# An attention kernel's filler scheduler: a work budget per step replaced by even rates for two engines

## The chip, the cores and the metric

One core of a Trainium2 chip. The metric is the device time of one launch of the whole program in microseconds, as the median of several runs. The engines are TensorE (PE in the profile; PEld is its weight load), VectorE (DVE), ScalarE (ACT), GpSimd (POOL) and SyncE (SP, whose queue SPq issues nearly all DMAs). Each engine runs its instructions in the order in which the program gives them.

## The reference

Two decoder layers over x of 4 batches, 512 tokens and 256 channels, each block added to x, with a second input ctx of 1024 tokens and 128 channels:

```python
x = x + L0_attn(ln(x))            # q, k softmaxed, 64 landmarks
x = x + L0_xattn(ln(x), ctx)      # (softmax(causal qk) v + softmax(cross qk) v) @ Wp
x = x + L0_ffn(ln(x))             # linear, x and W rounded to 6-bit floats in blocks of 32
x = x + L1_attn(ln(x))            # hyperbolic: -arccosh(..)^2 scores, causal, spike mask
x = x + L1_xattn(ln(x), ctx)      # y = ln(x); y += mha(y, y, causal); y = ln(y); y + mha(y, ctx)
x = x + L1_ffn(ln(x))             # 8 experts, top 2 of a softmax gate
# mha: 16 heads of 32; x + o @ li1, then + gelu(ln(.) @ li2) @ li3
```

In L0_xattn the heads are 16 wide. In L1_xattn the causal mask is laid on after the softmax, so its row sums run over all keys. The gate takes the two largest of 8 experts per token, and normalises their two scores.

## The kernel before, in words

Tokens lie on the 128 partitions, in 16 tiles for all batches; NT = 4 tiles per batch. The stages follow one another: L0_attn and the preparation of ctx (to about 200 us), **stream 0** (l0_xattn, L565), the hyperbolic attention (l1_attn, L985), **stream 1** (l1_xattn, L1210), the expert slots (Slots, L1656), and a last gather and sum.

Both streams are run by class Stream (L305). It has a list of units: one unit is four heads of one batch and one kind of attention, 32 units in each stream. A unit has two passes, both made of tiles of 128 by 512 scores in PSUM. In the first, the d tiles (d_tile, L355), TensorE computes scores with queries on the partitions (L363) and VectorE takes their row maxima (L367, L371, L375); for units marked norm ScalarE also sums exponentials (L379). In the second, the a tiles (a_tile, L394), TensorE computes the scores again, transposed and with the maxima taken in (a bias matmul, L391, or a changed query), and ScalarE writes the exponentials (L399). One step later the outputs multiply them by the values (L491 to L501). A step t is four heads of one d tile of one unit and one a tile of an earlier unit. Stream 0's units are cross attention (full) and causal; stream 1's are causal ones of the first block (marked norm; their mask is laid by GpSimd on the exponentials, L413) and full ones of the second. PSUM is a ring of seven score tiles and one output tile.

**Other work** is laid between the steps: everything that prepares a unit (layer norms ln_pieces, transposes flip, projections feats and values) or follows from one. In stream 0 that is also L0_ffn and the front of the hyperbolic attention (class Front, L737: scaled, binade, nearest and ties round to 6 bits; tokens L867 are the q, k, v projections; squares L888 to series L937 are cosh and sinh by exponentials and a power series on VectorE; lift L951 and turn L955 transpose them, and SP stores them for the next stage). In stream 1 it is li1, mid, flip, li2 (eight pieces), gelu and li3 (four pieces) of each batch and block, then leave, and from leave a gate chain per batch (gate, L1531: scores, choose, choose2, choose3, rank, four scatters of two indirect DMAs each on GpSimd (L1624), biases). After the last unit it is the first expert slots.

A piece is a tuple (earliest step, due step, least number of steps after the one before it, cost, function), and pieces stand in chains, which keep their order. In a step, `run` (L503) does in this order: force (L346) lays all pieces that are due, then come the step's tiles and outputs, then the functions put off by `after` (L324), then fill (L339) lays ready pieces, earliest due first, as long as the costs spent in this step are under a budget: 1.8 in stream 0 and 3.0 in stream 1, roughly microseconds of TensorE. What force laid counts; what `after` laid does not. Most of Front's VectorE pieces cost 0.

**Slots.** 39 slots of 128 routed tokens. Slot s needs its weights (2052 KB, fetch_w L1776) and its rows (fetch_z L1770); the rows of slots 0 to 15 (NEARLY) are loaded ahead, those of later slots in fetch. Four weight buffers. round (L1832) gives for each slot s: fetch(s + 3) with cost 0, two halves of hidden(s + 1), turn(s + 2), output(s) with a store on SP. The chain of slots 13 and later, which begins with fetch(16), is added by `rest` (L1404), just behind the scatters of the last gate, due at 10**6:

```python
s.chain([(s.t, 10**6, 0, c, f) for c, f in slots.rest()])          # L1405
if s + 3 < NSLOT:
    work.append((0.0, lambda s=s: self.fetch(s + 3)))
```

## Time and profile before

| | |
|---|---|
| median of 3 runs | 3500.57 us (3499.15 to 3501.44) |
| profiled execution, its own time | 3504.81 us |
| its span, first to last instruction | 3503.1 us |
| mean granted TensorE clock | 0.910 of full |
| VectorE, ScalarE, GpSimd busy | 2115.4, 1902.3, 781.9 us |
| stream 0, 200 to 1143 us: PE, DVE, ACT, POOL busy | 913.9, 664.3, 468.6, 154.6 us |
| stream 1, 1715 to 3133 us: PE, DVE, ACT, POOL busy | 1332.0, 855.6, 867.3, 204.1 us |
| slots, 3133 to 3450 us: PE busy, DMA share | 312.4 us, 0.76 |
| weights of a slot, issue to landing | 7.5 / 9.0 / 16.2 us (least, median, most) |

How to read it. A busy line gives an engine's busy time, its share of the span and its instructions. The rows of slices cut the span in 40 equal parts, one digit each, the busy share in tenths; PEclk is the clock that TensorE was granted, in tenths. The chain that ended last is followed back from the last instruction, and its shares say on which engine the time was spent. A timeline row has start, duration, engine, line, operation, output and inputs, and in brackets the idle time of the engine just before it and what released it. A line "x8" is eight instructions taken together, and matmuls of one row overlap, since their ends are modelled.

### The profile page before, as it was taken

What the parts mean: (1) busy time and instruction counts of PE and PEld (TensorE: products, weight loads), DVE (VectorE), ACT (ScalarE), POOL (GpSimd) and SP (SyncE); (2) the same over time, 40 slices, a digit from 0 to 9 for tenths busy, and PEclk for the clock granted to TensorE, in tenths of its full rate; (3) what the DMA queues carried; (4) which work ended last, traced back from release to release, by engine and by line L of the source; (5) the groups of instructions that cost most, each with busy time, mean ns of one, the idle gap of its engine ahead of it and who ended that gap; (6) DMA issues with size and microseconds to landing.
All of it is one profiled execution on the core that took longest, in us unless ns stands there. A gap on an engine that the chain in (4) does not pass through costs nothing.

```text
span 3503.1 us, 50666 instructions
## 1 busy us (share of the span) xinstructions
PE 3081.6 (88%) x19095; PEld 1514.7 (43%) x19095; DVE 2115.4 (60%) x5076; ACT 1902.3 (54%) x3845; POOL 781.9 (22%) x667
## 2 busy tenths in 40 slices
PE   6789999999999667677899989999999998989994
PEld 3433333333333334344434444433343343448994
DVE  4576676776776687876667564565657656433112
ACT  2225555454454765779587676556555664533331
POOL 1010112112122665668211220110101101021003
PEclk9779999999999667788789999999999999989997
DMA  8100000000000200020000000000000000035885
GB/s 281 57 26 7 1 7 1 14 24 4 28 1 14 71 13 32 25 98 7 25 1 1 1 1 19 7 1 31 1 13 9 11 1 13 7 145 203 317 328 166
DMA packets 81397, 176.08 MB, mean 50 GB/s; under 512 B 6264, under 2 KB 63744, under 8 KB 76032
## 3 DMA queue, kind: packets, MB, share of 16 engines
q1 hardware_dynamic: 76016, 161.16, 13.0%
q0 software_dynamic: 3072, 8.39, 0.8%
q8 instruction: 150, 2.46, 0.3%
q10 hardware_dynamic: 2064, 3.29, 0.3%
q14 instruction: 95, 0.78, 0.1%
HBM read 127.48 MB, written 45.34 MB: 49 GB/s over the span
## 4 chain that ended last, share of the span: by engine, by line
PE 67%; DVE 13%; ACT 10%; issue 5%; POOL 3%; DMA 3%; SPq 0%; POOLq 0%; ACTq 0%; DVEq 0%
PE ps_s L363 16%; PE ps_g L494 7%; PE ps_s L398 5%; PE ps_s L1802 4%; PE ps_s L1809 4%; PE ps_s L1401 3%; PE ps_s L1331 3%; PE ps_s L1385 3%; PE ps_s L636 3%; PE ps_s L391 2%; ACT pt L399 2%; ACT ps_s L379 2%; PE ps_s L1120 2%; PE ps_s L1372 2%; PE ps_g L501 2%
## 5 line engine op out<-in xcount | busy, mean ns | idle before, releaser
L399 ACT ACTIVATE pt<-ps_s 128x512 f32<-128x512 f32 (+2 forms) x1536 | 791.3, 570 | 758.8 <-PE ps_s L398 645.0
L363 PE MATMUL ps_s<-kT,qT 32*128 32x512 f32 (+3 forms) x3072 | 941.0, 633 | 38.1 <-ACT pt L399 12.7
L375 DVE TENSOR_REDUCE mx<-ps_s 128x1 f32<-128x512 f32 x768 | 490.4, 685 | 239.8 <-PE ps_s L363 136.8
L363 PEld LDWEIGHTS ps_s<-kT,qT 32*128 32x128 f32 x3072 | 322.9, 189 | 337.8 <-issue 121.8
L398 PE MATMUL ps_s<-qa,kT 32*128 32x512 f32 (+3 forms) x1536 | 447.9, 604 | 3.1 <-DVE mx L375 1.7
L367 DVE TENSOR_REDUCE mx<-ps_s 128x1 f32<-128x512 f32 x512 | 328.4, 685 | 166.1 <-PE ps_s L363 162.8
L398 PE MATMUL ps_s<-qT,kT 32*128 32x512 f32 x1536 | 421.9, 642 | 0.0
L379 ACT ACTIVATE ps_s<-ps_s,mx 128x512 f32<-128x512 f32 x512 | 341.2, 670 | 33.5 <-DVE mx L367 33.1
L1080 POOL TENSOR_TENSOR s<-s,mh 128x1280 f32<-128x1280 f32 x64 | 187.1, 2948 | 68.3 <-ACT mh L1079 52.4
L1804 ACT ACTIVATE hid<-ps_s,we 128x128 f32<-128x128 f32 x312 | 89.0, 370 | 199.0 <-issue 103.8
L164 POOL TENSOR_TENSOR ln_r<-ln_ve,mhalf 128x4 f32<-128x4 f32 x40 | 41.0, 1024 | 620.1 <-DVE ln_ve L159 556.4
L371 DVE CUSTOM_DVE_ANT_0 junk<-ps_s,dmask 128x512 f32<-128x512 f32 (+3 forms) x256 | 125.7, 491 | 88.2 <-PE ps_s L363 44.9
L391 PE MATMUL ps_s<-qm,all 3*128 3x512 bf16 x768 | 164.3, 391 | 12.6 <-ACT ps_s L379 10.8
L398 PEld LDWEIGHTS ps_s<-qa,kT 32*128 32x128 f32 x1536 | 148.8, 189 | 51.5 <-DVE mx L375 30.9
L1063 PE MATMUL ps_s<-qk 32*128 32x256 f32 (+3 forms) x512 | 102.2, 601 | 64.3 <-DVE mh L1068 57.5
L1802 PE MATMUL ps_s<-zsT,we 128*128 128x128 f32 x1248 | 149.2, 279 | 7.4 <-DVE zsT L1793 6.5
L1802 PEld LDWEIGHTS ps_s<-zsT,we 128*128 128x128 f32 x1248 | 147.9, 195 | 10.9 <-DVE zsT L1793 7.4
L1095 POOL TENSOR_TENSOR s<-s 128x1280 f32<-128x1280 f32 x64 | 147.6, 2339 | 12.3 <-ACT s L1091 12.3
L1120 PE MATMUL ps_s<-ident,s 128*128 128x128 f32 x640 | 129.1, 339 | 19.0 <-ACT s L1114 17.9
L1122 DVE COPY pt<-ps_s 128x512 f32<-128x512 f32 x160 | 108.6, 689 | 56.4 <-PE ps_s L1120 56.2
L1809 PE MATMUL ps_s<-we,hid 128*128 128x256 f32 x624 | 141.0, 379 | 0.0
L494 PE MATMUL ps_g<-pt,v 128*32 128x512 f32 x1024 | 140.4, 619 | 0.0
(439 smaller groups left out, 5096.9 us busy)
## 6 DMA issues: line engine op xcount, KB each, us to landing
we<-in_we SPq DMA_DIRECT2D x39, 2052.0 KB, 9.0
rows<-zero SPq DMA_DIRECT2D x8, 2048.0 KB, 17.0
qk_d<-qkT SPq DMA_DIRECT2D x32, 256.0 KB, 2.5
qk<-qk_d SPq DMA_DIRECT2D x8, 1024.0 KB, 6.6
zs<-rows SPq DMA_DIRECT2D x39, 128.0 KB, 3.7
outs<-ys SPq DMA_DIRECT2D x39, 128.0 KB, 3.7
li<-in_a_li SPq DMA_DIRECT2D x4, 1024.0 KB, 8.2
v_d<-vp SPq DMA_DIRECT2D x16, 143.5 KB, 1.8
```

The costliest lines, as they stand in the source:

```text
L363: PE.matmul(ps[:, 0:n], u.qT[r, ts(qt)], u.kT[r, hf * 512 : hf * 512 + n], start=True, stop=True)
L367: V.tensor_reduce(m, ps[:, 0:n], AX.X, ALU.max, negate=True)
L375: V.tensor_reduce(m, ps[:, 0:n], AX.X, ALU.max)
L379: S.activation(ps, ps, AF.Exp, bias=m, accum_out=sm)
L391: PE.matmul(ps, self.ones[r, :], u.qm[r, :], start=True, stop=False)
L398: PE.matmul(ps[:, c0:], u.kT[r, ts(kt)], (u.qa if u.first_row else u.qT)[r, c0:], start=u.first_row, stop=True)
L399: S.activation(u.pt[:, j, c0:], ps[:, c0:], AF.Exp, scale=u.scale)
L494: PE.matmul(o[r, c0:], u.v(kt, j), pt[:, j, c0:], start=first, stop=last)
L1080: G.tensor_add(s, s, m)
L1120: PE.transpose(ps[:, ts(j)], u.s[h // 2][:, h % 2, c0 : c0 + P], ident)
L1802: PE.matmul(ps[:, ts(f)], u.w[:, k : k + P], u.zT[:, c, :], start=c == 0, stop=c == 1)
L1809: PE.matmul(ps[:, 0:C], u.h[:, f, :], u.w[:, 2048 + f * C : 2048 + f * C + C], start=f == 0, stop=f == 7)
```

## The change

The budget is gone. A cost now has a sign: positive is microseconds of TensorE, negative of VectorE. At each step with score tiles, rates computes for each of the two engines the largest of (work due by d) / (steps to d + 1) over all due steps d; in steps without score tiles both rates are 3.0. fill lays a ready piece if it costs 0, if its engine has spent nothing in this step, or if half of it still fits under its engine's rate. force and `after` count what they lay. chain pulls the due steps of earlier pieces back to those of later ones. The costs are set anew (Front's VectorE pieces get theirs; scores from 2.0 to 3.4; scatter from 0.2 to 0), many due steps change: kT halves one step apart, the li1 to li3 chain by a lag and a pace, the gate's by 0.7 of a step per piece starting two steps earlier. hT6, the gate's transposed input, gets a buffer of its own instead of that of nT5. No computation changes. The core of the diff:

```diff
-        def __init__(self, jobs, budget, **kw):
+        def __init__(self, jobs, **kw):
             self.__dict__.update(kw)
-            self.jobs, self.budget = jobs, budget
+            self.jobs = jobs
...
-        def after(self, steps, fn):
-            self.later.setdefault(self.t + steps, []).append(fn)
+        def after(self, steps, fn, cost=0.0):
+            self.later.setdefault(self.t + steps, []).append((cost, fn))
 
 
         def chain(self, items, spill=False):
+            items = [[*i] for i in items]
+            for i, j in zip(items[-2::-1], items[:0:-1]):
+                i[1] = min(i[1], j[1])
             self.chains.append(SimpleNamespace(items=deque(items), at=-99, spill=spill))
...
-            return cost
-
-        def fill(self, spent):
-            while spent < self.budget:
-                ready = [c for c in self.chains if max(c.items[0][0], c.at + c.items[0][2]) <= self.t]
+            self.spent[cost < 0] += abs(cost)
+
+        def rates(self):
+            rates = [0.0, 0.0]
+            due = sorted((i[1], i[3]) for c in self.chains for i in c.items if i[3])
+            work = [0.0, 0.0]
+            for d, cost in due:
+                k = cost < 0
+                work[k] += abs(cost)
+                rates[k] = max(rates[k], work[k] / (max(d - self.t, 0) + 1))
+            return rates
+
+        def fill(self):
+            rates = self.rates() if self.t in self.d_at else [3.0, 3.0]
+            while True:
+                ready = [
+                    c for c in self.chains
+                    if max(c.items[0][0], c.at + c.items[0][2]) <= self.t
+                    and self.room(rates, c.items[0][3])
+                ]
                 if not ready:
                     return
-                spent += self.lay(min(ready, key=lambda c: c.items[0][1]))
+                self.lay(min(ready, key=lambda c: c.items[0][1]))
+
+        def room(self, rates, cost):
+            k = cost < 0
+            return not cost or self.spent[k] == 0.0 or self.spent[k] + abs(cost) / 2 <= rates[k]
 
         def force(self):
-            spent = 0.0
             while True:
                 due = [c for c in self.chains if c.items[0][1] <= self.t]
                 if not due:
-                    return spent
-                spent += self.lay(min(due, key=lambda c: c.items[0][1]))
+                    return
+                self.lay(min(due, key=lambda c: c.items[0][1]))
...
-            self.after(1, lambda: self.place(u, nm))
+            self.after(1, lambda: self.place(u, nm), 0.5)
...
-                spent = self.force()
+                self.spent = [0.0, 0.0]
+                self.force()
...
-                for f in self.later.pop(t, ()):
+                for cost, f in self.later.pop(t, ()):
                     f()
-                self.fill(spent)
+                    self.spent[0] += cost
+                self.fill()
...
-                            ctx_.append((f - 5, f - 3, False, 0.9, lambda u=u, h=h, g=g, cols=cols: feats(
+                            ctx_.append((f - 5, f - 4 + h, h, 0.9, lambda u=u, h=h, g=g, cols=cols: feats(
                                 u, "kT", wc["ck"], 1, cols, 1, bq[:, 12 + g : 13 + g], h, TC)))
-                        own.append((f - 5, f - 2, True, 1.7, lambda u=u, g=g, cols=cols: feats(
+                        own.append((f - 7, f - 2, True, 1.7, lambda u=u, g=g, cols=cols: feats(
...
-            return e, [(1, 0.5, scaled), (1, 0.5, binade), (1, 0.5, nearest), (1, 0.5, ties)]
+            return e, [(1, -3.0, scaled), (1, -1.4, binade), (1, -0.7, nearest), (1, -1.6, ties)]
...
-                work.append((1, 0.0, lambda t=t: squares(t)))
-            work += [(0, 0.0, norm), (apart, 0.0, spikes), (0, 0.0, roots), (1, 0.0, spikes2), (0, 0.0, norm2)]
-            work += [(apart, 0.0, power), (1, 0.0, cosh)]
-            work += [(1, 0.0, lambda: series(e.e, [1 / 3628800, 1 / 40320, 1 / 720, 1 / 24, 1 / 2], e.tm))]
-            work += [(1, 0.0, lambda: series(e.ei, [1 / 362880, 1 / 5040, 1 / 120, 1 / 6], e.sh)), (0, 0.0, halves)]
+                work.append((1, -1.2, lambda t=t: squares(t)))
+            work += [(0, -0.3, norm), (apart, 0.0, spikes), (0, 0.0, roots), (1, -0.3, spikes2), (0, -1.5, norm2)]
+            work += [(apart, 0.0, power), (1, -2.0, cosh)]
+            work += [(1, -1.5, lambda: series(e.e, [1 / 3628800, 1 / 40320, 1 / 720, 1 / 24, 1 / 2], e.tm))]
+            work += [(1, -1.3, lambda: series(e.ei, [1 / 362880, 1 / 5040, 1 / 120, 1 / 6], e.sh)), (0, -0.3, halves)]
             for t in range(NT):
-                work += [(1, 0.0, lambda t=t: lift(t)), (1, 1.5, lambda t=t: turn(t))]
+                work += [(1, -0.8, lambda t=t: lift(t)), (1, 0.9, lambda t=t: turn(t))]
...
-                                lambda: one.tile([P, 2, T], F32, name="hT6", tag="nT5"), ring,
+                                lambda: one.tile([P, 2, T], F32, name="hT6", tag="hT6"), ring,
...
-                            s.chain([(s.t, s.t + 4 + i, gap, c, f) for i, (gap, c, f) in enumerate(g)])
+                            s.chain([(s.t, s.t + 2 + int(0.7 * i), gap, c, f) for i, (gap, c, f) in enumerate(g)])
...
-                    work += [(1, 1.5, p) for p in ln_pieces(e.xo, z3)]
+                    work += [(1, -1.2, p) for p in ln_pieces(e.xo, z3)]
                     work += [(0, 0.0, mid), (True, 0.5, lambda: flip(e.z3, 0, [(e.nT, 8)]))]
                     work += [(False, 0.5, lambda: flip(e.z3, 1, [(e.nT, 8)]))]
                     work += [(f == 0, 1.7, lambda f=f: li2(f)) for f in range(8)]
-                    work += [(True, 0.1, gelu)]
+                    work += [(True, 0.0, gelu)]
                     work += [(t == 0, 3.4, lambda t=t: li3(t)) for t in range(4)]
                     work += [(False, 0.0, leave)]
 
-                    pace = 1 if (k, b) == (0, 0) else 3
-                    s.chain([(t0, t0 + (1 if i < 4 else pace + i - (i > 8)), gap, c, f) for i, (gap, c, f) in enumerate(work)])
+
+                    lag, pace = {(0, 0): (1, 1.0), (0, B - 1): (3, 1.1), (1, B - 2): (2, 0.65)}.get((k, b), (3, 1.0))
+                    s.chain([
+                        (t0, t0 + (1 if i < 4 else lag + int(pace * (i - (i > 8)))), gap, c, f)
+                        for i, (gap, c, f) in enumerate(work)
+                    ])
...
-                            oth.append((f - 4, f - 3, True, 0.9, lambda u=u, g=g, h=h: feats(u, "kT", g, h)))
+                            oth.append((f - 4, f - 3 + h, h, 0.9, lambda u=u, g=g, h=h: feats(u, "kT", g, h)))
...
-            [(2, 1.5, p) if i == 0 else (1, 1.5, p) for i, p in enumerate(ln_pieces(xb, z))]
-            + [(0, 0.0, begin), (1, 0.5, lambda: flip(0)), (0, 0.5, lambda: flip(1)), (1, 2.0, scores)]
-            + [(1, 1.5, choose), (1, 1.5, choose2), (1, 1.5, choose3), (1, 1.5, rank)]
-            + [(t == 0, 0.2, lambda t=t: scatter(t)) for t in range(NT)]
+            [(2 if i == 0 else 1, -1.2, p) for i, p in enumerate(ln_pieces(xb, z))]
+            + [(0, 0.0, begin), (1, 0.5, lambda: flip(0)), (0, 0.5, lambda: flip(1)), (1, 3.4, scores)]
+            + [(1, -1.5, choose), (1, -1.2, choose2), (1, -1.2, choose3), (1, 0.5, rank)]
+            + [(t == 0, 0.0, lambda t=t: scatter(t)) for t in range(NT)]
```

More of the change, by code (lines that the diff above doesn't have):

```diff
@@ L459, in last @@
                 self.split(nm.rearrange("p t (j s) -> p t j s", s=32), m)
-                self.after(1, lambda: self.place(u, nm))
+                self.after(1, lambda: self.place(u, nm), 0.5)
         def split(self, nv, m):
@@ L550, in run @@
                             S.copy(o, acc)
-                            self.after(1, lambda u=u, o=o: u.done(o))
+                            self.after(1, lambda u=u, o=o: u.done(o), 0.5 if u.first_row else 0.0)
                 prev = None
@@ L600, in l0_xattn @@
             s = Stream(
-                list(jobs.values()), 1.8, ptp=ptp, op=wk, one=one, qap=qap, nms=nms, dmask=dmask
+                list(jobs.values()), ptp=ptp, op=wk, one=one, qap=qap, nms=nms, dmask=dmask
             )
@@ L669, in finish @@
                     if g == 3:
-                        s.after(2, lambda: project(0))
-                        s.after(3, lambda: project(1))
+                        s.after(2, lambda: project(0), 0.5)
+                        s.after(3, lambda: project(1), 0.5)
                         for t in range(NT):
-                            s.after(5 + t, lambda t=t: project(2 + t))
+                            s.after(5 + t, lambda t=t: project(2 + t), 0.9)
                 def project(k):
@@ L692, in batch @@
                 f0 = jobs[b, True, 0].first_d
-                own = [(f0 - 18, f0 - 12 + i, 1, 1.0, p) for i, p in enumerate(ln_pieces(xb, z))]
+                own = [(f0 - 18, f0 - 12 + i, 1, -1.2, p) for i, p in enumerate(ln_pieces(xb, z))]
                 own += [
@@ L812, in turn @@
                 V.tensor_copy(self.wT, ps.rearrange("p (c n) -> p c n", n=C))
-            return work + [(1, 1.0, turn)]
+            return work + [(1, 0.5, turn)]
         def batch(self, b, alone=False):
@@ L843, in norm_pieces @@
             def norm_pieces(z):
-                return [(1 + apart * (i == 2), 1.0, p) for i, p in enumerate(ln_pieces(xb, z))]
+                return [(1 + apart * (i == 2), -1.2, p) for i, p in enumerate(ln_pieces(xb, z))]
             work = norm_pieces(z1)
@@ L1256, in l1_xattn @@
             s = Stream(
-                list(jobs.values()), 3.0, tail=lambda: tail(), ptp=ptp, ptmp=wk, op=one, qap=qmp, nms=nms, ones=ones, identb=identb,
+                list(jobs.values()), tail=lambda: tail(), ptp=ptp, ptmp=wk, op=one, qap=qmp, nms=nms, ones=ones, identb=identb,
                 onesf=onesf,
@@ L1447, in block @@
                 for i, p in enumerate(first):
-                    own.append((fr, max(fr, f0 - 17) + i, 1, 1.5, p))
+                    own.append((fr, max(fr, f0 - 17) + i, 1, -1.2, p))
                 own.append((f0 - 20, f0 - 13 + k, 0, 0.0, enter))
                 for i, p in enumerate(second):
-                    own.append((f0 - 20, f0 - 10 + i, 2 if i == 0 else 1, 1.5, p))
+                    own.append((f0 - 20, f0 - 10 + i, 2 if i == 0 else 1, -1.2, p))
                 own += [(f0 - 20, f0 - 7, 0, 0.0, begin)]
@@ L1459, in block @@
                     if k == 0:
-                        own.append((f - 4, f - 3, True, 1.7, lambda u=u, g=g: feats(u, "kT", g, 0)))
+                        own.append((f - 5, f - 3, True, 1.7, lambda u=u, g=g: feats(u, "kT", g, 0)))
                     else:
```

## The prediction

> **What bounds the kernel now.** I read the page first: the busy line, the slices, the chain that ended last.
>
> ```profile
> PE 3081.6 (88%) x19095; PEld 1514.7 (43%) x19095; DVE 2115.4 (60%) x5076; ACT 1902.3 (54%) x3845; POOL 781.9 (22%) x667
> PE   6789999999999667677899989999999998989994
> PEclk9779999999999667788789999999999999989997
> PE 67%; DVE 13%; ACT 10%; issue 5%; POOL 3%; DMA 3%; SPq 0%; POOLq 0%; ACTq 0%; DVEq 0%
> ```
>
> TensorE sets the time. The table by stage splits it: stream 0 from 200 to 1143 us (PE busy 914 of 943), the hyperbolic attention to 1715 (393 of 572, untouched), stream 1 to 3133 (1332 of 1418), the expert slots to 3450 (312 of 317). So nothing is won by starting TensorE's work earlier as such; only where its records are stretched by waits or a slow clock, or where it idles. The timeline of TensorE in stream 0 shows how other work meets a step:
>
> ```profile
> 464.91 1.06 PE L494 MATMUL ps_g<-pt,vc 128*32 128x512 f32 x8
> ...
> 468.86 1.07 PE L494 MATMUL ps_g<-pt,vc 128*32 128x512 f32 x8
> ...
> 470.93 1.13 PE L686 MATMUL ps_s<-w2p,yT 128*128 128x256 f32 x4
> 471.90 0.60 PE L473 MATMUL ps_s<-ident,nm 128*128 128x128 f32 x4
> ...
> 473.50 1.07 PE L494 MATMUL ps_g<-pt,vc 128*32 128x512 f32 x8
> ```
>
> From one output group to the next is 3.95 us with nothing laid between and 4.64 with 1.30 us of TensorE work (0.86 + 0.44). I measured this period P at every step against the TensorE work W between. Full tiles of stream 0 follow P = max(3.95, 3.34 + W): at W = 1.72, 5.05; 3.44, 6.78. Below 3.95 a step waits for VectorE's maxima (4 of 0.685 us, group L375), since the ring has seven score tiles. So **the first 0.61 us of W per step is hidden, the rest is exposed**. In stream 1's norm steps it is max(4.7, 3.7 + W): about 1.0 hidden. Its steps that mix full and norm tiles are between 0 and 1.0, its full ones without norm hide nothing.
>
> The rest of what a scheduler can reach is waits. Two of them, in the timeline:
>
> ```profile
> 2084.33 2.34 POOL L1190 TENSOR_TENSOR x<-x,bc 128x1024 f32<-128x1024 f32 x1
> ...
> 2086.70 0.43 DVE L155 BATCH_NORM_STATS2 ln_st<-x 128x6 f32<-128x256 f32 x1 [5.55 <-POOL x L1190]
> ...
> 2089.85 1.22 PE L363 MATMUL ps_s<-kT,qT 32*128 32x512 f32 x2 [5.61 <-DVE hT L1389]
> ```
>
> VectorE stood 5.55 us behind GpSimd's affine (enter), and TensorE 5.61 behind VectorE. The sum over all steps of measured period less the law is 42 us in stream 0 and 118 in stream 1.
>
> **The change, part by part.** The built program has the same instructions in both versions (19095 matmul records' worth, the same table loads): this is order alone, plus one buffer given a tag of its own. I took the order of both built programs and put W through the fitted law, transition by transition.
>
> *Evening TensorE's pieces.* Stream 0 has 238 us of W in both. Of its steps with full tiles on both sides, 35 had almost none before and 22 have after; those with two pieces or more fall from 19 to 7. The law's sum up to step 186 falls 15 us. Stream 1 has 752 us of W, largely li2 and li3 put one per step where two stood together: the law's sum falls 18 us. Check by count: stream 0's hidden W rises from 73 to 89.
>
> *Stream 0's last steps.* The last but one batch's front (tokens L867 to turn L955) slips by about six steps into steps without score tiles. Steps 187-191 lose 10.3 us of token matmuls (four of 2.58), which come back exposed at 193-196; turns 0-3 then run at 202-209 with no score tiles, about 2.8 us a pair, beside the projections. From step 186 to the last turn the trace has 67.5 us (1080.0 to 1147.5); mine is 42.6 + 28 = 70.6. **+3**. First load of the hyperbolic stage is queued on SP behind that turn's store, so this counts in full.
>
> *VectorE bursts of stream 0.* cosh, series and the first turns cost 10.6 us over the law at steps 99-105, and similar at 147-153. After, two steps instead of one separate series and turn and other steps take them. I give half of it in one batch, **-5**; scaled, binade and nearest stay where they are. Bounds -15 and +5.
>
> *Waits of stream 1.* Affine then statistics (above, steps 54-55): 8.5 us; after, enter is forced at step 52 with four normalisation pieces (VectorE 7.3 us at once), the next statistics two steps on: about half stays, -4. gelu then li3 at step 77-78: 4.3 us lost since gelu (3.62 us, two table loads of 1.28) stood one step ahead; after, five steps ahead: -4. Steps 68 and 83 (mid, and leave ahead of a normalisation): -1.5 and -4. The other six gelu waits (3 to 6 us each) stay one step apart, so stay. New: choose3 and rank are forced together ahead of li1 at steps 144 and 177 (and in the tail), so TensorE meets VectorE's chain of 2-3 us: +4. The scatters of the gates (8 of 2.67 us on GpSimd) move behind yT and ahead of the next normalisation: the 16.8 us lost at 173-182 takes another form and stays. The last gate starts one step earlier and its scatters, which the slots' first loads wait for, come about 5 us earlier: -5. Sum **-15**, bounds -40 and +5.
>
> *The expert slots' loads.* This is the part against the change. A piece of cost zero now always finds room. The chain of the later slots (rest) begins with fetch(16), of cost zero; before, the budget was spent and it came at step 250, after fetch(15). After, it is issued in step 233, right after fetch(8). It has two parts on SP's queue: the rows of slot 16, which wait for the last of the 32 scatters, then 2.05 MB of weights. Behind it on the same queue stand the output store of slot 5 and the weights of slots 9, 10, 11. The scatters before:
>
> ```profile
> 3211.79 0.96 POOL L1624 DMA_INDIRECT rows<-ln_z,idx  x1 [5.89 <-DVE past L1706]
> 3218.80 0.96 POOL L1624 DMA_INDIRECT rows<-ln_z,idx  x1 [6.05 <-DMA rows<-ln_z,idx]
> 3224.75 0.96 POOL L1624 DMA_INDIRECT rows<-ln_z,idx  x1 [4.99 <-DMA rows<-ln_z,idx]
> 3227.41 0.96 POOL L1624 DMA_INDIRECT rows<-ln_z,idx  x1 [1.70 <-DMA rows<-ln_z,idx]
> ...
> 3250.57 0.96 POOL L1624 DMA_INDIRECT rows<-ln_z,idx  x1 [6.95 <-DMA rows<-ln_z,idx]
> ```
>
> Beside weights in flight a scatter takes 6 to 8 us, between two loads 2.67. With the loads held, the remaining five after 3217 run at 2.67: last landing about 3233. Then slot 16's weights go at 3234.5 and slot 9's at 3236. TensorE is done with slot 8 at 3232.69 (before's clock) and wants slot 9:
>
> ```profile
> 3232.69 3.73 PE L1802 MATMUL ps_s<-zsT,we 128*128 128x128 f32 x32
> ```
>
> One load lands in 7.5 / 9.0 / 16.2 us (least, median, most; the most where three were issued at once), so slot 9's lands at about 3249: **a stall of 16 us**. By the Trainium skill's "DMA: Bandwidth & Descriptors", Specifications, a core's share of HBM is 358 GB/s, so 4.2 MB would need 11.7 us and 3248.5; the trace moved 411 GB/s in 3128-3132, which would give 10.2 and 3247. The row decides, and I keep 16. Moreover slot 16 holds one of four weight buffers seven slots early: slots 11 to 15 are loaded one slot (7.25 us) ahead and not two, against 7.5 to 9.0 to land: 0.3 to 1.8 us each, +4. The Trainium skill's "TensorE: Matmul & The Clock Gate", Part 1, has the array fall to half rate after an idle window of about 3.4 us; the trace agrees that it does (granted 0.50 in 3112-3116 after a gap) and that it stays for multiples of 3.41 us: by the row +3, without the rule 0. Sum **+23**, bounds +12 and +50 (scatters all at 7.5 us).
>
> *The tag of hT6* takes a wait on nT5 away; the gate's transposes come long after li2, so 0.
>
> **Sum.** -15 + 3 - 5 - 18 - 15 + 23 = -27 us. The profiled execution took 3504.81 us (span 3503.1), 4.2 more than the median 3500.57; taking 27 from the median gives 3474.
>
> **Rivals.**
> *The clock.* Stream 1 spends some 140 us at half rate in windows of 3.4 to 10.2 us, stream 0 some 58: up to 99 us lost. If a denser TensorE keeps half of stream 1's windows away beyond those I counted: -35, so 3439. For it: windows follow stalls (2310-2314 at 0.50 after the wait of step 83). Against: those at steps 8, 12 and 16 (3 us each) follow step ends that hardly change.
> *The evening brings half.* VectorE's pieces are now laid in the same steps as TensorE's (cosh in a full step beside a projection), and the free room exists only while VectorE is on time: the evening -17 instead of -35 (-15 + 3 - 5 - 18), waits -7, loads +23: -1, 3500.
> *Slower: the held queue.* The price of fetch(16) is SP's stop until the last scatter. If the scatters keep 7.5 us each, the last lands at 3265, slot 9 at 3281, a stall of 48, +55 in all. From a price of 50 (35 + 15) the sum changes sign; with half the evening's gain it is 55 - 17 - 15 = +23, 3523.
> *It doesn't do what it says.* The order shows that it does, with forced pieces in stream 1 at 52, 144 and 153.
>
> **How the numbers follow.** My case 0.50 (3455-3493), the clock 0.20, half the evening 0.12, the held queue 0.18. The range 3438 to 3512 leaves about 0.2 out. About 0.2% (7 us) is what a measurement tells from no change. Faster by more 0.70, within 0.12, slower 0.18. Predicted 3474.
>
> **What would show it.** Right: in the changed profile one idle stretch of TensorE of 12-20 us ahead of slot 9's hidden layer, SP's row load of slot 16 right after slot 8's weights, scatters at 2.7 us; stream 0 shorter by 15-20 us up to the hyperbolic stage, stream 1 by 30-35 up to the first slot. Wrong: no such stretch, or scatters at 7 us; a stream 0 that ends no earlier; gelu waits gone at all eight MLPs.

## The result, and the profile after

The changed kernel takes 3510.28 us (median; 3505.88 to 3515.18) beside 3499.85 us (3496.88 to 3503.32) of the kernel before: ratio 1.0031, 95% interval 1.002 to 1.0041. It is about 10 us slower, where 27 us faster was forecast. Its profiled execution took 3505.88 us with a span of 3504.0, 0.9 more than before's span.

The page after, the four lines that answer to those of before:

```profile
PE 3055.5 (87%) x19095; PEld 1489.4 (43%) x19095; DVE 2107.0 (60%) x5076; ACT 1901.9 (54%) x3845; POOL 781.5 (22%) x667
...
PE   6689999999998576677899999999998998987994
...
PEclk9789999999999567777899999999998999999997
...
PE 66%; DVE 13%; ACT 7%; issue 7%; DMA 5%; POOL 2%; SPq 0%; ACTq 0%; DVEq 0%; POOLq 0%
```

TensorE is busy 26 us less for the same instructions (3081.6 before): its records are less stretched, by waits or by a slow clock; the busy line doesn't say by which. Two things are worse: two of the last ten slices of the PE row have an 8 (from 2628 us) and a 7 (from 3154 us) where there was a 9, and DMA's share of the chain went from 3 to 5%.

The two traces laid over each other, by the time at which the same work starts (for a step, its second half):

| place | before | after | difference |
|---|---|---|---|
| stream 0, step 186 | 1082.9 | 1057.7 | -25.2 |
| stream 0, step 192 (no d tiles from here) | 1111.0 | 1083.5 | -27.5 |
| first scores of the hyperbolic stage | 1156.6 | 1142.8 | -13.8 |
| stream 1, step 0 | 1722.3 | 1711.1 | -11.2 |
| stream 1, step 132 | 2640.0 | 2589.8 | -50.2 |
| stream 1, step 191 | 3055.2 | 3043.3 | -11.9 |
| first rows of the slots asked for | 3114.1 | 3093.3 | -20.8 |
| slot 9's hidden layer | 3232.7 | 3226.9 | -5.8 |
| end of the span | 3503.1 | 3504.0 | +0.9 |

So 50 us were won, more than the forecast had for both streams together, and given back at three places: 14 at the end of stream 0, 38 between steps 132 and 191 of stream 1, and 22 between the slots' first rows and the end.

**The steps in stream 0.** TensorE's timeline, from one output group to the next:

```profile
440.28 1.06 PE L517 MATMUL ps_g<-pt,vc 128*32 128x512 f32 x8
...
444.86 1.07 PE L517 MATMUL ps_g<-pt,vc 128*32 128x512 f32 x8
...
449.06 1.06 PE L517 MATMUL ps_g<-pt,vc 128*32 128x512 f32 x8
...
451.12 0.66 PE L706 MATMUL ps_s<-ident,y 128*128 128x128 f32 x4
...
453.01 1.07 PE L517 MATMUL ps_g<-pt,vc 128*32 128x512 f32 x8
```

The third period carries a transpose of 0.6 us and takes 3.95, the time of an empty step: hidden, as the law has it. The first, with 1.3 us laid, takes 4.58 (4.64 before).

**Affine and statistics in stream 1.** GpSimd's and TensorE's timelines at step 52, which answer to the wait shown at 2084:

```profile
2050.91 2.34 POOL L1214 TENSOR_TENSOR x<-ln_z,bc 128x1024 f32<-128x1024 f32 x1 [2.29 <-DVE ln_z L192]
2053.34 2.34 POOL L1215 TENSOR_TENSOR x<-x,bc 128x1024 f32<-128x1024 f32 x1
```

```profile
2052.30 3.78 PE L1356 MATMUL ps_s<-xnT,wq 128*128 128x512 f32 x4 [4.35 <-ACT ps_s L402]
```

The step is 6.5 us longer than the law gives, before two steps were 8.5: -2 for the predicted -4.

**GpSimd's scatters in stream 1.** The largest new wait, step 180. GpSimd's, VectorE's and TensorE's timelines:

```profile
2943.58 0.96 POOL L1653 DMA_INDIRECT rows<-ln_z,idx  x1 [1.70 <-DMA rows<-ln_z,idx]
2946.25 0.96 POOL L1653 DMA_INDIRECT rows<-ln_z,idx  x1 [1.72 <-DMA rows<-ln_z,idx]
2947.24 1.04 POOL L164 TENSOR_TENSOR ln_r<-ln_ve,mhalf 128x4 f32<-128x4 f32 x1
2948.27 2.33 POOL L1402 TENSOR_TENSOR x<-x,xo 128x1024 f32<-128x1024 f32 x1
2950.67 2.35 POOL L1403 TENSOR_TENSOR x<-x,bc 128x1024 f32<-128x1024 f32 x1
```

```profile
2941.27 0.17 DVE L159 TENSOR_SCALAR ln_ve<-ln_mv 128x4 f32<-128x4 f32 x1
...
2948.31 2.31 DVE L169 TENSOR_TENSOR ln_t<-ln_r 128x4 f32<-128x4 f32 x1 [4.99 <-POOL ln_r L164]
2950.65 0.16 DVE L170 TENSOR_TENSOR ln_t<-ln_t,ln_ve 128x4 f32<-128x4 f32 x1
2950.85 2.20 DVE L171 TENSOR_SCALAR ln_t<-ln_t 128x4 f32<-128x4 f32 x1
```

```profile
2955.54 2.07 PE L1356 MATMUL ps_s<-cn,wk 128*128 128x512 f32 x2 [9.45 <-ACT ps_s L402]
```

VectorE had the variance at 2941.4. The power (L164, 1.04 us) stood behind the scatters until 2947.2, since each holds the queue for 2.67. Then the second half: L169 and L171 are 128x4 operations of 0.15 to 0.17 us that took 2.31 and 2.20. They end at 2950.62 and 2953.05, which is where mid's two additions on GpSimd end (2950.60, 2953.02). TensorE's bracket names ScalarE, but ScalarE itself had waited 9.81 us for VectorE's maxima (L390), and these stood behind all this:

```profile
2954.71 0.66 ACT L402 ACTIVATE ps_s<-ps_s,mx 128x512 f32<-128x512 f32 x1 [9.81 <-DVE mx L390]
```

**gelu.** ScalarE's timeline at step 163:

```profile
2818.57 1.28 ACT L1417 ACT_TABLE_LOAD   x1
2819.86 3.62 ACT L1417 ACTIVATE hT<-hT 128x4096 f32<-128x4096 f32 x1
2823.49 1.28 ACT L1418 ACT_TABLE_LOAD   x1
2824.79 1.09 ACT L422 ACTIVATE pt<-ps_s 128x512 f32<-128x512 f32 x2
```

6.2 us without exponentials, in a step where ScalarE has exponentials for both tiles: with sums for the d tile (L402) and for the a tile (L422). Here gelu and li3 cost 9.0 us more than the prediction's law gives for the step ("over the law" below); before, gelu stood at step 158, where the d tile has no sums, and the pair cost 3.2.

**The slots.** SP's queue and TensorE:

```profile
3186.08 0.35 SPq L1809 DMA_DIRECT2D we<-in_we  x1
3211.42 0.35 SPq L1803 DMA_DIRECT2D zs<-rows  x1
3212.60 0.34 SPq L1809 DMA_DIRECT2D we<-in_we  x1
...
3214.26 0.34 SPq L1809 DMA_DIRECT2D we<-in_we  x1
```

```profile
3208.37 3.62 PE L1838 MATMUL ps_s<-we,hid 128*128 128x256 f32 x16
3226.89 5.67 PE L1831 MATMUL ps_s<-zsT,we 128*128 128x128 f32 x32 [14.90 <-DMA we<-in_we]
```

Slot 16's rows (L1803) stand right behind slot 8's weights and hold SP for 25 us until the last scatter has landed; slot 9's weights follow at 3214.26, and TensorE idles 14.90 us. The scatters in that time, on GpSimd, 2.67 us apart:

```profile
3206.32 0.96 POOL L1653 DMA_INDIRECT rows<-ln_z,idx  x1 [1.71 <-DMA rows<-ln_z,idx]
3209.00 0.96 POOL L1653 DMA_INDIRECT rows<-ln_z,idx  x1 [1.72 <-DMA rows<-ln_z,idx]
```

**The end of stream 0.** TensorE's timeline, the last batch but one's turns (L986) among the last projections:

```profile
1121.98 1.97 PE L986 MATMUL ps_s<-ident,hy 128*128 128x128 f32 x8 [2.85 <-DVE hy L978]
...
1124.80 1.10 PE L986 MATMUL ps_s<-ident,hy 128*128 128x128 f32 x8
...
1127.82 1.07 PE L986 MATMUL ps_s<-ident,hy 128*128 128x128 f32 x8 [1.48 <-DVE hy L978]
...
1131.31 1.06 PE L986 MATMUL ps_s<-ident,hy 128*128 128x128 f32 x8 [0.70 <-DVE hy L978]
...
1142.84 2.09 PE L1088 MATMUL ps_s<-qk 32*128 32x512 f32 x8 [8.74 <-DMA qk<-qk_d]
```

Three of the four wait for their lift on VectorE, 5.0 us together. From step 186 to the end of the last turn it is 74.7 us (1057.7 to 1132.4), before 63.1 (1082.9 to 1146.0). To the last output group (step 202) both need the same, 60.6 and 61.3 us; behind it the changed kernel has 15.1 us to the end of the last turn, the one before 2.8. The rates don't hold these pieces back: the change tests for d tiles, so from step 192 on both rates are 3.0, though a tiles still come.

### The profile page after: what moved, and what is told of

Its sections match the earlier page's. It is cut to its first block, busy times and chain, and to the rows that moved or that the text cites. A ratio compares the mean times of both kernels' runs of the same rounds, so it can differ in the third digit from the quotient of the medians.

```text
span 3504.0 us, 50650 instructions
## 1 busy us (share of the span) xinstructions
PE 3055.5 (87%) x19095; PEld 1489.4 (43%) x19095; DVE 2107.0 (60%) x5076; ACT 1901.9 (54%) x3845; POOL 781.5 (22%) x667
## 4 chain that ended last, share of the span: by engine, by line
PE 66%; DVE 13%; ACT 7%; issue 7%; DMA 5%; POOL 2%; SPq 0%; ACTq 0%; DVEq 0%; POOLq 0%
PE ps_s L386 16%; PE ps_g L517 7%; PE ps_s L421 5%; PE ps_s L661 3%; PE ps_s L1831 3%; PE ps_s L1838 3%; PE ps_s L1410 3%; PE ps_s L1356 3%; PE ps_s L1426 3%; PE ps_s L414 2%; PE ps_s L1145 2%; PE ps_g L524 2%; DMA rows<-ln_z,idx 1%; PE ps_s L1367 1%; DMA we<-in_we 1%
## 5 line engine op out<-in xcount | busy, mean ns | idle before, releaser
L422 ACT ACTIVATE pt<-ps_s 128x512 f32<-128x512 f32 (+2 forms) x1536 | 791.0, 569 | 749.0 <-PE ps_s L421 647.8
L386 PE MATMUL ps_s<-kT,qT 32*128 32x512 f32 (+3 forms) x3072 | 921.9, 623 | 45.6 <-ACT pt L422 28.0
L386 PEld LDWEIGHTS ps_s<-kT,qT 32*128 32x128 f32 x3072 | 310.9, 186 | 338.5 <-issue 96.4
L390 DVE TENSOR_REDUCE mx<-ps_s 128x1 f32<-128x512 f32 x512 | 328.3, 684 | 194.1 <-PE ps_s L386 190.9
L421 PE MATMUL ps_s<-qa,kT 32*128 32x512 f32 (+3 forms) x1536 | 436.0, 590 | 4.9 <-ACT pt L422 3.1
L402 ACT ACTIVATE ps_s<-ps_s,mx 128x512 f32<-128x512 f32 x512 | 340.9, 670 | 32.8 <-DVE mx L390 32.3
L1831 PE MATMUL ps_s<-zsT,we 128*128 128x128 f32 x1248 | 148.8, 278 | 22.7 <-DMA we<-in_we 20.6
L414 PE MATMUL ps_s<-qm,all 3*128 3x512 bf16 x768 | 156.6, 387 | 5.8 <-ACT ps_s L402 3.1
L164 POOL TENSOR_TENSOR ln_r<-ln_ve,mhalf 128x4 f32<-128x4 f32 x40 | 40.8, 1020 | 538.4 <-DVE ln_ve L159 476.0
L1093 DVE TENSOR_SCALAR_CACHE_REDUCE mh<-ps_s 128x512 f32<-128x512 f32 (+3 forms) x256 | 108.5, 486 | 53.1 <-PE ps_s L1092 28.8
```

Of the source, the lines that this page charges most:

```text
L386: PE.matmul(ps[:, 0:n], u.qT[r, ts(qt)], u.kT[r, hf * 512 : hf * 512 + n], start=True, stop=True)
L390: V.tensor_reduce(m, ps[:, 0:n], AX.X, ALU.max, negate=True)
L402: S.activation(ps, ps, AF.Exp, bias=m, accum_out=sm)
L414: PE.matmul(ps, self.ones[r, :], u.qm[r, :], start=True, stop=False)
L421: PE.matmul(ps[:, c0:], u.kT[r, ts(kt)], (u.qa if u.first_row else u.qT)[r, c0:], start=u.first_row, stop=True)
L422: S.activation(u.pt[:, j, c0:], ps[:, c0:], AF.Exp, scale=u.scale)
```

## The experiments

The theory: evening is right and worth about 50 us, and three things give it back: the front's late end, stream 1's pieces that the new due steps put beside the wrong neighbours (scatters ahead of a power, VectorE's products beside GpSimd's, gelu among sums), and the held queue. The rivals stand with each run. "Over the law" is a step's measured period less the law of the prediction. A difference to the changed kernel "by the ratio" is the run's ratio less 1.0031, times 3503; "by the spans" it is the run's span less 3504.0.

| run | median us | ratio to before | 95% interval | span of its trace |
|---|---|---|---|---|
| s0_only | 3496.7 | 0.9977 | 0.9967 to 0.9987 | 3495.2 |
| rest_late | 3490.4 | 0.9965 | 0.9953 to 0.9977 | 3485.4 |
| scat_spread | 3501.6 | 0.9991 | 0.9981 to 1.0 | 3499.6 |
| drain | 3505.61 | 1.0011 | 1.0001 to 1.0021 | 3503.5 |
| before_fetch | 3525.59 | 1.0068 | 1.0055 to 1.0082 | 3523.9 |
| pace | 3476.08 | 0.9926 | 0.9913 to 0.994 | 3473.0 |
| gate_due | 3502.75 | 1.0006 | 0.9997 to 1.0014 | 3497.6 |
| combo1 | 3446.36 | 0.9839 | 0.9826 to 0.9852 | 3446.7 |
| bias_late | 3503.38 | 0.9991 | 0.998 to 1.0002 | 3503.6 |
| combo2 | 3443.06 | 0.9819 | 0.9802 to 0.9836 | 3445.4 |
| after_again | 3513.44 | 1.0027 | 1.0017 to 1.0037 | 3502.7 |
| before_gelu | 3498.9 | 0.9985 | 0.9974 to 0.9996 | 3499.9 |

**Stream 0 alone.** Two stream classes; stream 1, its gate and the slots from the kernel before.

```diff
-            s = Stream(
+            s = StreamOld(
```

> Stream 0 with the new scheduler, costs and due steps; stream 1, its gates and the expert slots with the old ones. Theory: stream 0's evening is worth 27 us up to its last steps with score tiles, 14 to 16 of which are lost at its end, so stream 1 starts 11 us earlier and nothing behind it changes: 11 us faster than before (3489), ratio 0.997. Rival: what stream 0 gains is only borrowed (work put off) and all is paid back by its end: 0, 3500. A third outcome, that the changed start shifts the clock windows of the later stages, would show as a gain other than 11 with the difference made behind 1700 us.

Ratio 0.9977, -8 us (0.0023 of 3504). Its trace has stream 0's step 192 at -24.4, stream 1's step 0 at -7.7 and every later step at -7.7. The theory holds (11 us lie within the interval, 8 is what came), and the first rival does not. The gain is won and lost within stream 0: the later steps run exactly as before.

**The held queue, from both sides.** In the changed kernel, the later slots' chain waits for step 250; in the kernel before, slot 16 is asked for as early as the changed kernel does.

```diff
-                        s.chain([(s.t, 10**6, 0, c, f) for c, f in slots.rest()])
+                        s.chain([(s.t + 17, 10**6, 0, c, f) for c, f in slots.rest()])
```

```diff
-                        s.chain([(s.t, 10**6, 0, c, f) for c, f in slots.rest()])
+                        work = slots.rest()
+                        work[0][1]()
+                        s.chain([(s.t, 10**6, 0, c, f) for c, f in work[1:]])
```

> The changed kernel, with the chain of the later slots held back until step 250, so that slot 16's rows and weights are asked for behind slot 15's and not behind slot 8's. Theory: the held queue costs 22 us in the changed kernel (stop ahead of slot 9's hidden layer 15, one slot of lead less for slots 11 to 15 and the clock 7), and all of it goes: 22 us faster than the changed kernel (3488), 12 faster than before, no idle stretch of TensorE over 5 us ahead of slot 9. Rival: the weights are short anyway (DMA share 0.76 among the slots in the kernel before) and the stop moves to a later slot: under 8 us faster than the changed kernel (3502 or more).

> The kernel before, in which only slot 16's rows and weights are asked for where the changed kernel asks for them (behind the last gate's scatters, ahead of slot 9's weights), all else unchanged. Theory: the held queue is worth 22 us by itself, whatever the scheduler: 22 us slower than before, ratio 1.006, one idle stretch of TensorE of about 15 us ahead of slot 9's hidden layer. Rival: in the kernel before, the scatters overlap with loads in flight and end at 3257, so that the queue would be held longer: 40 us or more. Second rival: the price depends on the changed kernel's denser order of slots: under 10 us.

Against the changed kernel's 1.0031 rest_late is 0.0066 lower, -23 us; before_fetch is +24. TensorE's timeline at slot 9, first rest_late, then before_fetch:

```profile
3218.70 3.62 PE L1838 MATMUL ps_s<-we,hid 128*128 128x256 f32 x16
3222.16 3.73 PE L1831 MATMUL ps_s<-zsT,we 128*128 128x128 f32 x32
```

```profile
3246.54 3.75 PE L1804 MATMUL ps_s<-zsT,we 128*128 128x128 f32 x16 [17.57 <-DMA we<-in_we]
```

No gap in the one, 17.57 us in the other. The queue costs 22 to 24 us under either scheduler. Both rivals of before_fetch and the one of rest_late fall.

**The front drawn together.**

```diff
-                            s.chain([(s.t + 1, s.t + 4 + i, gap, c, f) for i, (gap, c, f) in enumerate(work)], spill=True)
+                            pace = 0.8 if b == B - 2 else 1
+                            s.chain([(s.t + 1, s.t + 4 + int(pace * i), gap, c, f) for i, (gap, c, f) in enumerate(work)], spill=True)
```

> The changed kernel, with the due steps of the front of stream 0's last but one batch drawn together to 0.8 of a step per piece, so that its token projections start four steps earlier. Theory: the end of stream 0 loses 14 us because that front's chain of VectorE pieces and turns runs on after the last score tile; with it earlier the hyperbolic stage starts 6 to 9 us earlier: 3503. Rival: the end of stream 0 is set by the last unit's own projections and by the load that follows, and the earlier pieces only fill steps: within 3 us (3507 to 3513).

The hyperbolic stage starts at 1135.1, 7.8 us earlier than in the changed kernel, as the theory has it. But stream 1 starts only 2.4 earlier: the stage took 573 us and not 568, in jumps of 1 to 3 us along it. The edit doesn't touch that stage, and behind the changed kernel's stream 0 it takes 564.1 to 570.9 us in the eight traces without this edit, so some of it may be chance. By the ratio it is -7, by the spans -0.5. The mechanism is shown, what of it reaches the end is not settled.

**The scatters apart.** For the first two gates, scatters two steps apart and the pieces behind them later.

```diff
+                            late = [0] * n + ([0, 2, 4, 6, 6, 6, 6] if b < B - 2 else [0] * 7)
+                            s.chain([
+                                (s.t, s.t + 2 + int(0.7 * i) + late[i], 2 if b < B - 2 and n < i < n + 4 else gap, c, f)
```

> The changed kernel, with the scatters of the first two gates laid two steps apart instead of all eight DMAs in one step, and the pieces behind them six steps later. Theory: eight scatters in a row hold GpSimd for 21 us, the layer norm's power and the affine of the next batch stand behind them and then meet VectorE's small products on the port; the waits at steps 146, 151, 152 and 180 (together 28 us over the law) fall to 10: 15 to 20 us faster than the changed kernel (3492). Rival: it is VectorE's normalisation pieces, forced together, and not the scatters: within 4 us of the changed kernel (3506 to 3514), with TensorE still waiting over 5 us at steps 146 and 180.

Over the law at step 146: 8.2 to under 1; at 180: 14.2 to 3.7; at 151 and 152: 6.1 to 9.1. From step 144 to 191 13 us faster than the changed kernel, and -14 by the ratio: a little under what was expected. At step 180 the cause is confirmed: the power now runs at 2949.3, between the second DMA (2936.3) and the third (2950.5). At step 146 it is not, since the edit moves the biases too; the next run takes them alone.

**Only the biases later.**

```diff
+                            if b == 0:
+                                g[-3] = (5, *g[-3][1:])
+                            s.chain([
+                                (s.t, s.t + 2 + int(0.7 * i) + 5 * (b == 0 and i > len(g) - 4), gap, c, f)
```

> The changed kernel, with only the first gate's biases (three small products on VectorE, then transposes) laid four steps later, at 150 instead of 146; the scatters and the affine stay where they are. Theory: at step 146 it is not GpSimd's queue that TensorE waits for, but VectorE's three small products, which took 2.9 and 2.3 us instead of 0.2 since GpSimd's affine ran at the same time; moved, they take 0.15 to 0.3 us, and the 8 us over the law at step 146 fall below 2: 6 to 8 us faster than the changed kernel (3503). Rival: the backlog of scatters on GpSimd is what the step waits for: over 5 us stay at steps 146 to 150, and the time is within 3 us.

VectorE's timeline at step 146 of the changed kernel, then the same operations in this one (two products in one row, then their sum):

```profile
2705.87 3.02 DVE L1661 TENSOR_TENSOR go<-go,wt 128x32 f32<-128x32 f32 x2
2708.92 2.27 DVE L1662 TENSOR_TENSOR gp<-go,go 128x32 f32<-128x32 f32 x1
```

```profile
2736.14 0.29 DVE L1666 TENSOR_TENSOR go<-go,wt 128x32 f32<-128x32 f32 x2
2736.47 0.19 DVE L1667 TENSOR_TENSOR gp<-go,go 128x32 f32<-128x32 f32 x1
```

5.3 us became 0.5, with the same backlog of scatters on GpSimd. In the changed kernel the affine's two operations ran there at the same time:

```profile
2706.38 2.35 POOL L1214 TENSOR_TENSOR x<-ln_z,bc 128x1024 f32<-128x1024 f32 x1
2708.80 2.34 POOL L1215 TENSOR_TENSOR x<-x,bc 128x1024 f32<-128x1024 f32 x1
```

Step 146 is within 1 us of the law; 3.9 us come up at step 150, where the biases now stand beside a normalisation. Steps 144 to 156 are 6.4 us faster, as expected; the whole is -14 by the ratio and -0.4 by the spans, and 6 to 8 lies between the two. So the rival falls by what step 146 shows; the times alone would not decide it.

**The gate's due steps as before the change**, for the first two gates.

```diff
+                            early = b >= B - 2
+                                (s.t, s.t + (2 + int(0.7 * i) if early else 4 + i), gap, c, f) for i, (gap, c, f) in enumerate(g)
```

> The changed kernel, with the gate's due steps of the first two batches as before the change (4 + 1 step per piece, not 2 + 0.7). Theory: choose3 and rank are no longer forced ahead of li1 (8.5 us over the law at steps 142 and 143), the affine of step 146 comes ahead of the scatters (8 us), and the 14 us at step 180 go; new is that the third buffer of the layer norm is asked for while the scatters of step 151 still read the one before: up to 15 us at step 153. Net 10 to 15 us faster than the changed kernel (3498). Rival: the gate's due steps do not matter, since the same pieces meet the same engines a few steps later: within 4 us.

Steps 142, 143 and 146 fall to the law (from 16.7 over) and 180 from 14.2 to 4.7, but step 152 has 23.7 over. VectorE's timeline there:

```profile
2748.93 3.37 DVE L192 TENSOR_SCALAR ln_z<-xo,ln_mv,ln_r 128x256 f32<-128x256 f32 x2 [17.43 <-DMA rows<-ln_z,idx]
```

The layer norm has two buffers, and the one that it wants is still read by the scatters. The place was expected, 15 us of it, not 24. By the ratio -9, a little under the theory's 10 to 15.

**The pace of two batches.** li1 to li3 of the second block's first two batches as the change has it for the third.

```diff
-                    lag, pace = {(0, 0): (1, 1.0), (0, B - 1): (3, 1.1), (1, B - 2): (2, 0.65)}.get((k, b), (3, 1.0))
+                    lag, pace = {(0, 0): (1, 1.0), (0, B - 1): (3, 1.1), (1, 0): (2, 0.65), (1, 1): (2, 0.65), (1, B - 2): (2, 0.65)}.get((k, b), (3, 1.0))
```

> The changed kernel, with the chain from li1 to li3 of the first two batches of the second block due at 2 + 0.65 of a step per piece (as the changed kernel already has it for the third batch) instead of 3 + 1. Theory: gelu then falls at steps 123 and 155, which have few exponentials, and no longer at 130 and 163, where ScalarE is full: 18 us over the law become 7; the gates come six steps earlier, clear of li1, of the next batch's affine and of its power: the 40 us over the law at steps 135 to 152 and 176 to 181 become about 15; TensorE's pieces stand two to a step again, 4 us. Sum 30 us faster than the changed kernel (3480). Rival: gelu's two table loads and the gate's pieces cost the same wherever they stand, and only the evening is lost: 0 to 4 us slower than the changed kernel.

-37 us against the changed kernel, -31 by the spans. Steps 135 to 182, gelu left out: 48.5 us over the law become 10.3. The two gelu and li3 pairs: 17.9 become 10.4, where 7 was expected. The rival falls.

**gelu by itself**, in the kernel before: two steps later.

```diff
-                    work += [(True, 0.1, gelu)]
+                    work += [(3 if (k, b) == (1, 1) else True, 0.1, gelu)]
```

> The kernel before, with only the gelu of one batch (second block, second batch) held back by two steps, from 158 to 160, and so into steps in which both score tiles carry exponentials with sums; li3, leave and that batch's gate come two steps later with it. Theory: the wait of gelu and li3 rises from 3 to 9 us over the law, and the gate's scatters, now behind li1 at step 177 and ahead of the power of step 179, make TensorE wait 10 us or more at steps 178 to 181, in place of the 13 us of steps 174 to 177: together 4 to 8 us slower than before. Rival: gelu costs 3 us wherever it stands, and the scatters are hidden there: 0 to 10 us faster.

gelu and li3 went from 3.2 over the law to 8.4 (6.2 and 2.2): the theory's 9. Its second half failed: the gate's scatters, two steps later, cost 4.3 us (steps 178, 179) and not 10; before they cost 13. They began at 2934 and ended at 2957, and the power ran at 2959.9, behind them anyway. In the kernel before it is not a power that stands behind them, but the second half of yT, for which li1 then waits 4.70 us on TensorE:

```profile
2941.46 0.96 POOL L1624 DMA_INDIRECT rows<-ln_z,idx  x1 [1.72 <-DMA rows<-ln_z,idx]
2942.45 0.87 POOL L1361 TENSOR_TENSOR yT<-o 128x128 f32<-128x128 f32 x2
```

Two steps later yT comes ahead of the scatters. So the net is -5 us by the ratio to before (-3.2 by the spans), which lies in the rival's range, though its reason (gelu costs the same wherever it stands) is wrong. What counts is whether GpSimd work that TensorE will soon need stands behind scatters, and two steps decide it.

**Together.** combo1 is rest_late, drain and pace; combo2 also lays li3 and leave of two batches two steps later.

```diff
+                        due[-5:] = [d + 2 for d in due[-5:]]
+                        work[-5] = (1 + 2, *work[-5][1:])
```

> The changed kernel with three of the edits together: the later slots' chain held back to step 250, the front of stream 0's last but one batch drawn together, and the pace of the second block's first two batches. Theory: the three act at different places and add: 22 + 7 + 30 = 59 us faster than the changed kernel, 48 faster than before (3452), ratio 0.986. Rival: what is won in the streams is lost at the slots, whose loads then start earlier but end no earlier (DMA share 0.76 among them): 20 us faster than before.

> The three edits together (the later slots' chain held back, the front drawn together, the pace of the second block's first two batches), and li3 and leave of these two batches two steps later, so that TensorE no longer comes to li3 one step behind gelu. Theory: gelu costs 6.2 us of ScalarE, and what TensorE loses by it depends on the step that it stands in and on how soon li3 follows: the two waits of 5.2 us ahead of li3 at steps 124 and 156 go: 8 us faster than without this edit (3438), ratio 0.981. Rival: gelu holds up ScalarE's exponentials and so the steps wherever it stands, and two waits of 4 to 6 us appear at the steps of gelu itself: within 3 us of the kernel with the three edits (3446).

combo1 is 57 us under the changed kernel by the spans and 67 by the ratios (59 expected): the edits add. The clock goes with it: 0.920 granted in both combos and 0.917 in pace, 0.914 in the changed kernel's trace. combo2's further edit is not told apart: the waits before li3 (5.2 each) came up at gelu's own steps (3.2 and 4.9), as its rival said, and the intervals overlap. Both beat the kernel before by 1.5% and more. Two lines of combo2's page:

```profile
PE 3045.9 (88%) x19095; PEld 1492.0 (43%) x19095; DVE 2104.2 (61%) x5076; ACT 1901.4 (55%) x3845; POOL 782.4 (23%) x667
...
PEclk8789999999999667777799999999999999999997
```

**Once more the changed kernel.**

> The changed kernel once more, nothing edited. What is open: its median was 10 us above that of the kernel before, while the two traces differ by 1 us from end to end (3504.0 and 3503.1). Theory: the ten microseconds are 1 to 5 us of scheduling and the rest is what one execution differs from another: the ratio falls to 1.000 to 1.003, and the spans of the two traces of the changed kernel differ by several us at the same instructions. Rival: the first trace happened to be the fastest execution and misses a cost of the change: the ratio stays at 1.003, and the second trace shows where about 9 us more go.

Ratio 1.0027, span 3502.7; over stream 1 its trace lies 1 to 2 us from the first at the same steps and shows the same waits. So the 10 us are real, and both traces show one or none of them: both profiled executions (3505.88, 3504.64) are among the fastest of the changed kernel, while that of the kernel before (3504.81) is slower than all eight of the result. The other runs share stages with one kernel or the other, and their traces show what the first one missed (us; the middle one of the traces that run the stage in the same order, and their number):

| stage | before | changed, first trace | changed, all such traces |
|---|---|---|---|
| stream 0 to step 186 | 879.9 (3) | 856.1 | 856.2 (8) |
| to the first hyperbolic scores | 76.3 (3) | 87.2 | 87.5 (8) |
| hyperbolic stage | 565.2 (3) | 567.7 | 568.2 (8) |
| stream 1 to step 132 | 915.7 (4) | 877.1 | 880.3 (7) |
| from there to step 191 | 415.5 (3) | 453.6 | 453.6 (4) |
| to the end | 450.1 (3) | 462.8 | 461.8 (6) |

The last column's sum is some 3 us more than that of the first trace: steps 63 and 68 of stream 1 were shorter there, by 1.7 and 1.6 us. The rest goes with the granted clock: over the 12 executions of this run, and the 23 of the kernel before beside them, 0.001 less of it goes with 1.7 and 1.8 us more. The two traces had 0.914 and 0.916, where the middle of these executions is 0.909 (0.910 for the kernel before, as in its trace). At one clock, 0.912, the lines through the two sets stand 9 us apart. Why one execution is granted more than another no run shows, and for that reason a difference to the changed kernel by ratios is up to 9 us larger than by spans.

## Why the prediction was wrong

Its own steps, forecast and measured, between the two traces:

| step of the prediction | forecast | measured |
|---|---|---|
| evening of stream 0, to step 186 | -15 | -15.4 by the law |
| VectorE's bursts of stream 0 (measured: all its waits to step 186) | -5 | -9.8 |
| stream 0's last steps | +3 | +11.6 to the last turn |
| hyperbolic stage | 0 | +2.4 |
| evening of stream 1 | -18 | -20.6 by the law |
| waits of stream 1, to step 203 | -10 | +17.1 |
| last gate and scatters | -5 | -6.1 |
| the slots' loads | +23 | +21.7 |
| sum | -27 | +0.9 |

The rows "by the law" put the built order through the prediction's law; they are worked out, and the rows of waits are what is left. Measured are the sums: -25.2 for the first two rows, -9.6 for the three of stream 1. The hyperbolic stage's +2.4 is not told from nothing: with its code untouched it took 561.1 to 573.1 us in the traces.

**Right:** both evenings (steps 13 to 32 of the changed stream 0 lie on the law within 0.05 us where both tiles are full), the price and the place of the held queue (16 forecast, 14.90 in the trace; scatters at 2.67), the last gate, the built order. Two statements above need to be put right, though nothing rests on them: the 752 us of W "in stream 1" take in the slots' pieces to 3450 us (up to 3100 us the trace before has 439), and PSUM is a ring of seven score tiles and one output tile in stream 0 only; in stream 1 it is six and two.

The rivals. *The evening* did not bring half. *The scatters* did not keep 7.5 us, so the held queue alone did not reach its turning point of 50. *The clock* was not it, though the means (0.914 granted, 0.910 before) hide a move: 0.97 became 0.99 in stream 0 to step 186, 0.95 became 0.97 in stream 1 to step 132, and behind it 0.96 became 0.94 (0.99 in pace). In stream 1 this is some 123 us at half rate before and 109 after (twice what is missing to 1, times the stretch), worth 7 us at most, where the rival had 35. Nearly all stretches at half rate lie in steps that are over the law or just behind them (13.7 us in step 180 alone), so they are a part of what a wait costs, and no run takes the two apart.

That 3510 lies within the stated 3438 to 3512 is luck: the upper part of the range stood for rivals that did not come. The kernel is slower for another reason.

**The step that failed is "waits of stream 1": -15 with the last gate, measured +11.** To step 132 it was right (-15). Behind it 32 us came, mostly in two terms:

- "The other six gelu waits (3 to 6 us each) stay one step apart, so stay." The second block's four pairs went from 14.6 to 26.8 us over the law. li2 laid one per step ends later, and two gelus come six and five steps later (from 124 to 130, from 158 to 163), among exponentials with sums; before_gelu and pace show that this decides. The prediction looked at the distance from gelu to li3, not at what ScalarE does in that step.
- The gates, steps 135 to 182: "+4" for choose3 and rank, and the scatters' wait "takes another form and stays". Measured 25.3 before, 48.5 after. choose3 and rank are 8.5 of the 48.5 (a part mis-sized), 28.5 stand at steps 146, 151, 152 and 180, where scatters lie ahead of affine and power; scat_spread brings these four to some 13.5. Eight DMAs in a row are not new: the kernel before has them too (2922.7 to 2942.4), and so has pace. New is what stands behind them; and what they push together, GpSimd's wide additions and VectorE's small products, blocks one another, which the prediction did not count.

**Mis-sized:** stream 0's end, +3 forecast and +11.6 measured. Turns of 2.8 us a pair were about right (2.8 to 3.5 apart), but they were to run beside the projections: behind the last output group they and the last projections take 15.1 us with nothing to hide them, 5.0 of it waits for VectorE's lifts.

The forecast's -27 was taken from the median, and the medians differ by 9 us more than the two traces of the table: this adds to the miss, and only in part is it known where (the table of stages above).

## What to carry to other kernels

An even rate for two engines is worth having, but it only sees those two: where the third and fourth engines work in bursts (eight scatters, a gelu of 6.2 us), check for every moved piece what stands on their queues in its new step. A piece of cost zero is not free if work that another engine needs stands behind it on the same queue: give it a place, not a cost. Read a difference of two schedules as a running difference over the same steps; the end alone hid a gain of 50 us and three losses.

## What the runs showed of the hardware

A small VectorE operation can wait inside its own record and show no idle time: 0.15 to 2.31, 0.17 to 2.20, 0.19 to 2.27 us, each ending with a 2.3 us operation on GpSimd (lines above). The Trainium skill's "SBUF — State Buffer", Who interferes with whom, has the two engines share a pair of ports under an exclusive lock; of a VectorE operation in a two-port mode and one of GpSimd, the one that issues second "fully blocks" for the whole instruction, and operations with two inputs in SBUF contend as well. The trace agrees for these three: each started after GpSimd's operation and ended with it to within 0.1 us. The product of 2.9 us at step 146 ended with the affine too, but had started half a microsecond before it, while a scatter was being issued; what held it at first is not shown. Such operations are found by looking for records far longer than others of their line, not by the brackets. And a gate's eight scatter DMAs in a row on GpSimd are 21 us in which nothing else runs there: 2.67 each, 0.96 of issue and 1.7 of waiting.
